# A two-layer relational graph convolution: layer 1's result kept in SBUF, transposed sums, and x and the output in rows of eight nodes

## The chip, the cores and the metric

The kernel runs on one core of a Trainium2 chip. The metric is the device time of one execution in microseconds. The median of three runs of the kernel before is 4638.85 us (4636.51 to 4646.56).

The core has five engines with a queue of instructions each: TensorE (PE, matmuls and weight loads), VectorE (DVE), ScalarE (ACT), GpSimd (POOL) and SyncE (SP). Here POOL does hardly anything but issue indirect DMAs (gathers of rows named by an index list), and SP issues nearly all other DMAs.

## The reference

`x` has 12500 nodes of 128 features. There are 200000 edges, sorted by their target `dst`, each with a source `src` and one of 8 relations. Two layers of a relational convolution are followed by a residual and a layer norm:

```python
def _rgcn_conv(x, src, dst, et, basis, comp, root, bias):
    W = jnp.einsum('rb,bio->rio', comp, basis)
    xw = jnp.einsum('ni,rio->nro', x, W)
    msgs = xw[src, et]
    seg = dst * N_REL + et
    summed = jax.ops.segment_sum(msgs, seg, num_segments=N_NODES * N_REL)
    cnt = jax.ops.segment_sum(jnp.ones((msgs.shape[0],), x.dtype), seg, num_segments=N_NODES * N_REL)
    mean = summed / jnp.maximum(cnt, 1.0)[:, None]
    agg = mean.reshape(N_NODES, N_REL, HIDDEN).sum(axis=1)
    return agg + x @ root + bias
...
    h = x
    for l in range(N_LAYERS):
        h_new = _rgcn_conv(h, src, dst, edge_type, basis[l], comp[l], root[l], bias[l])
        h_new = jax.nn.relu(h_new)
        h = h_new + h
    return h
...
x = _layernorm(x + _L0_gnn_ref(x, edge_index, edge_type_8, L0_gnn_basis, L0_gnn_comp, L0_gnn_root, L0_gnn_bias), axis=-1)
```

So each edge brings its source's row, times the weight of its relation, divided by the number of edges of that relation at its target.

## The kernel before, in words

**The plan.** `ordered_path` does the work (`general_path` stands by for edges whose distribution the first can't take; a flag read at the end chooses). It records every operation in program order in a `Plan` (lines 300 to 399), with the cells that it reads and writes. The plan derives the semaphore waits from these, and emits each engine's operations in that order. Nothing reorders them later: an engine that waits holds up all that is behind it in its queue. DMAs of SP, of ACT and of POOL's gathers use small sets of lanes (8, 4 and 3), and a DMA waits for the one before it on its lane.

**Sizes.** Nodes come in 98 blocks of 128 (`NT`), the last of 84. Edges come in 1563 tiles of 128. Four tiles make a quad (`Q`, 391 of them), eight a group (`G`, 196). A block of nodes has about 16 tiles, that is four quads or two groups. All data is fp32. A gather fetches the rows of one tile, so a quad is four gathers. Gathers are issued 12 quads ahead (`AHEAD`) into a ring of 14 slots `rows`; one-hot matrices two quads ahead, into a ring `dm` of 4.

**Layer 0.** For each quad `q` in turn: `gather` rows of x for quad q + 12 (line 577); `onehot` for quad q + 2 on DVE (line 863); `means` (line 903): PE multiplies the gathered rows with the one-hots, which are already divided by the counts, and ACT copies the result to `sT`. At even quads `product` of the group before (line 927): 16 PE passes through the weights of the eight relations, copied by ACT to `ys`. At odd quads `place` (line 950): PE adds the rows of `ys` into the sums `po` of the one or two blocks that they belong to. The sum of a block is opened by the root matmul in `open_block` (line 889), whose operand is x transposed: `load_block` loads 128 rows of x (64 KB), `turn_block` transposes them (line 882, bank `pt`) and ACT copies them to `hT`. When a block is complete, `close_block` adds the bias (line 963), takes the relu and adds x (line 964), and puts three items on a list `todo`: `turn` transposes the result on PE (line 970, bank `pt`), ACT copies it to `y_col`, and SP stores it to the DRAM tensor `hT_d`; `half(0)` and `half(1)` multiply it with the layer 1 weights of four relations each (line 975, bank `pt`), ACT copies to `y_row`, and the second stores 512 KB to the DRAM table `y_d`, which has a row for every node and relation. One item is taken from the list at three quads of four.

**Between the layers.** Layer 1 gathers from `y_d`, by node and relation, so its first gather waits for all stores to `y_d`.

**Layer 1.** Since the table holds products already, a quad takes one step, `add_rows` (line 1016): PE multiplies gathered rows and 256 wide one-hots into a transposed sum for two blocks; the root matmul (line 1019) is in it. `load2` fetches for each block its layer 1 input from `hT_d` to `h_in`, and its rows of x to `xs`. After a block's last quad `finish` lets ACT carry the half that belongs to the next block (line 1028, with the bias), and DVE adds the carry from before (line 1035) and does relu and residual (line 1036). One quad later `norm` transposes the block back on PE (line 1050); DVE adds x (line 1051), takes mean and variance (lines 1052 and 1053), ACT the root (line 1054), DVE the reciprocal and the scaling (lines 1056 and 1057), and SP stores 64 KB of output.

Names of lines 562, 565 and 577 in the profile are helpers: all loads and stores, all ACT copies, and all gathers.

Of the kernel before, what the change touches and what calls it, by code (L numbers as in the profile page):

```python
# [401 lines left out]
class Ring:  # L402


    def __init__(self, pool, n, shape, dtype, name):
        self.name, self.at = name, 0
        self.tiles = [pool.tile(shape, dtype, name=f"{name}{i}") for i in range(n)]
# [8 lines left out]
def ordered_path(  # L416
# [12 lines left out]
):  # L429

# [33 lines left out]
    assert D == P and R * K == P and B == BF + 1 and 1 < TL and LAST < P and BF % 4 == 0  # L464
# [9 lines left out]
    hT_d = dram.tile([NT * P, P], F32, name="hT_d")  # L474
# [9 lines left out]
    bias_sb = keep([P, D], F32, "bias_sb")  # L484
    bias_t = keep([P, 1], F32, "bias_t")
# [7 lines left out]
    dx = keep([P, B, C], I32, "dx")  # L493
    ex = keep([P, B, C], I32, "ex")
    src_i = keep([P, B, P], I32, "src_i")
    comp_sb = keep([P, L * R * NB], F32, "comp_sb")
    b_sb = keep([P, L, NB, D], F32, "b_sb")
# [9 lines left out]
    key = keep([P, 4, C], F16, "key")  # L507
    low = keep([P, 4, C], I32, "low")
    eqs = Ring(const, 2, [P, S4, 4, C], F16, "eq")
    turns = Ring(const, 3, [P, 4, P], F32, "tu")  # L510
# [5 lines left out]
    hin_r = Ring(const, 5, [P, D], F32, "h_in")  # L516
    hT_r = Ring(const, 3, [P, P], F32, "hT")
    h_r = Ring(const, 3, [P, D], F32, "h")
    yc_r = Ring(const, 3, [P, P], F32, "y_col")
    yr_r = Ring(const, 2, [P, R, D], F32, "y_row")  # L520
    xs_r = Ring(const, 4, [P, D], F32, "xs")
    st_r = Ring(const, 3, [P, nc.vector.BN_STATS_DIM + nc.vector.BN_AGGR_DIM + 1], F32, "st")
# [4 lines left out]
    po_b = [(psum.tile([P, D], F32, name=f"po{i}"), ("po", i)) for i in range(2)]  # L527
# [5 lines left out]
    v1 = keep([P, P], F32, "v1")  # L533
    v2 = keep([P, P], F32, "v2")
    v3 = keep([P, P], F32, "v3")
# [33 lines left out]
    def gather(l, q):  # L569
# [14 lines left out]
        if l == 1 and q == 0:  # L584
            reads += [("y_d", j) for j in range(NT)]
# [37 lines left out]
    def start():  # L623
# [26 lines left out]
        load(bias_sb, bass.AP(tensor=bias.tensor, offset=bias.offset, ap=[[0, P], [1, D]]), [], ["bias"], "ACT")  # L650
        load(bias_t, bass.AP(tensor=bias.tensor, offset=bias.offset + D, ap=[[1, P], [1, 1]]), [], ["bias_t"], "ACT")
# [127 lines left out]
    def check_edges(b):  # L779
        dxc = [("dx", b), ("dx", b, 1), ("dx", b, 2), ("dx", b, 3), ("pad", "dx")]  # L780
        for emit, r, wr in (
            (lambda: nc.vector.tensor_tensor(v1, dx[:, b, HALO + 1:HALO + P + 1], dx[:, b, main], op=ALU.is_lt),
             dxc, "v1"),
            (lambda: nc.vector.tensor_tensor(v2, dx[:, b, 2 * HALO:2 * HALO + P], dx[:, b, main], op=ALU.subtract),
             dxc, "v2"),
# [84 lines left out]
    def load_block(j):  # L870
        if j >= NT:
            return
# [151 lines left out]
    def finish(k):  # L1024
# [4 lines left out]
        if k < 0:  # L1029
            return  # L1030
# [199 lines left out]
```

## Time and profile before

| | before |
|---|---|
| median of three runs | 4638.85 us |
| the profiled execution | 4641.11 us |
| its span, first to last instruction | 4639.3 us |
| gathers of layer 0 | 3.4 to 2328.4 us |
| gathers of layer 1 | 2379.7 to 4591.5 us |
| PE busy | 2355.8 us (51%) |
| DVE busy | 1697.2 us (37%) |
| ACT busy | 502.0 us (11%) |
| POOL busy | 2962.0 us (64%) |
| bytes moved | 295.75 MB |

A row of the groups reads: line, engine, operation, what it writes from what it reads, number; busy time and mean length in ns of one; idle time of the engine just before them and what ended most of it. A row of the waits reads: engine, what waited, what released it, line of that; total in us, number, longest. "issue" is a gap with no wait that the profile shows, "remote" one with a releaser that it does not know. Ends of matmuls are modelled.

### The profile page before, as it was taken

The page shows a single profiled execution, that of the slowest core. Times are in us where ns is not written, and L with a number is a line of the kernel's source. Part 1 is how long each engine was busy: PE and PEld are TensorE (multiplying, and loading weights), DVE is VectorE, ACT ScalarE, POOL GpSimd, SP SyncE. Part 2 cuts the span into 40 slices and gives each one's busy share as a digit, 9 for nine tenths or more (in the row PEclk, how much of TensorE's full clock was granted, in tenths as well). Part 3 has the DMA queues.
Part 4 walks back from the last instruction along what each step waited for, and adds up shares of the span by engine and source line. Part 5 has one row for each costly group of instructions (what it writes and reads, how often), then busy time and mean ns, then how long its engine had stood idle before and what let it go on. Part 6 is the DMA issues. An engine that isn't in the chain of part 4 may idle for free.

```text
span 4639.3 us, 34983 instructions
## 1 busy us (share of the span) xinstructions
PE 2355.8 (51%) x11691; PEld 1911.0 (41%) x11691; DVE 1697.2 (37%) x4724; ACT 502.0 (11%) x1190; POOL 2962.0 (64%) x3134
## 2 busy tenths in 40 slices
PE   1675565556655565565563443444444344444444
PEld 1454555455544554454442332333333233333333
DVE  3874222222222232232232343434334343434434
ACT  0121111111111111121110000000000000000000
POOL 5466666666666666666646666666666666666663
PEclk9998888788788877788876776777777776767677
DMA  2122222222222222222221111211111111111121
GB/s 79 37 71 74 75 75 74 74 75 75 74 74 74 75 79 73 72 79 74 70 69 51 55 56 54 57 55 56 54 56 56 55 56 56 54 55 56 54 57 37
DMA packets 193392, 295.75 MB, mean 64 GB/s; under 512 B 60725, under 2 KB 130687, under 8 KB 193203
## 3 DMA queue, kind: packets, MB, share of 16 engines
q0 software_dynamic: 100032, 205.07, 15.6%
q1 hardware_dynamic: 90650, 86.62, 5.8%
q8 instruction: 96, 1.57, 0.1%
q10 hardware_dynamic: 2521, 1.73, 0.1%
q14 instruction: 93, 0.76, 0.1%
HBM read 229.18 MB, written 64.00 MB: 63 GB/s over the span
## 4 chain that ended last, share of the span: by engine, by line
another core or an unknown queue 38%; PE 26%; DVE 17%; issue 14%; ACT 3%; POOL 2%; DMA 0%; POOLq 0%; DVEq 0%; ACTq 0%; SPq 0%
DVE dm L863 12%; PE s L903 8%; PE y L927 6%; PE pt L975 4%; PE po L950 3%; POOL rows L577 2%; PE s L1016 1%; ACT sT L565 1%; DVE w_sb L597 1%; PE ct L705 1%; DVE eq L699 1%; PE ct L706 1%; DVE st L1052 1%; DVE ys L1057 1%
## 5 line engine op out<-in xcount | busy, mean ns | idle before, releaser
L577 POOL DMA_INDIRECT rows<-in_x_dram,idx x1563 | 1485.4, 950 | 841.0 <-issue 420.5
L577 POOL DMA_INDIRECT rows<-y_d,idy x1563 | 1475.5, 944 | 787.6 <-issue 419.0
L1016 PE MATMUL s<-dm,rows 128*128 128x256 f32 x2086 | 646.0, 469 | 595.1 <-DVE dm L863 482.0
L863 DVE TENSOR_SCALAR dm<-cols,near,w 128x256 f32<-128x256 f32 x1563 | 727.0, 533 | 255.3 <-remote 185.9
L1016 PEld LDWEIGHTS s<-dm,rows 128*128 128x128 f32 x2086 | 487.6, 245 | 710.3 <-DVE dm L863 499.6
L863 DVE TENSOR_SCALAR dm<-cols,kr,w 128x128 f32<-128x128 f32 x1563 | 525.9, 401 | 569.3 <-remote 348.1
L903 PEld LDWEIGHTS s<-dm,rows 128*128 128x128 f32 x3126 | 470.9, 222 | 121.9 <-issue 115.4
L903 PE MATMUL s<-dm,rows 128*128 128x128 f32 x3126 | 485.5, 305 | 6.1 <-issue 5.1
L950 PE MATMUL po<-ys,pl 128*128 128x128 f32 x780 | 167.6, 349 | 628.3 <-ACT ys L565 467.6
L927 PE MATMUL y<-w_sb,sT 128*128 128x128 f32 x3136 | 439.5, 300 | 65.4 <-issue 43.3
L1016 PE MATMUL ct<-dm,rows 128*128 128x256 f32 x1040 | 314.6, 457 | 291.1 <-DVE dm L863 216.7
L927 PEld LDWEIGHTS y<-w_sb,sT 128*128 128x128 f32 x3136 | 422.8, 216 | 75.1 <-issue 48.8
L950 PEld LDWEIGHTS po<-ys,pl 128*128 128x128 f32 x780 | 131.1, 239 | 656.4 <-ACT ys L565 486.9
L1016 PEld LDWEIGHTS ct<-dm,rows 128*128 128x128 f32 x1040 | 235.2, 237 | 347.7 <-DVE dm L863 224.7
L963 DVE TENSOR_TENSOR h<-po,bias_sb 128x128 f32<-128x128 f32 x98 | 28.5, 291 | 872.3 <-PE s L903 281.2
L1051 DVE TENSOR_TENSOR h<-po,xs 128x128 f32<-128x128 f32 x98 | 27.9, 285 | 816.6 <-remote 731.7
L565 ACT ACTIVATE sT<-s 128x512 f32<-128x512 f32 x391 | 233.8, 598 | 838.5 <-PE s L903 466.3
L975 PE MATMUL pt<-w_sb,y_col 128*128 128x512 f32 x392 | 254.1, 736 | 55.2 <-issue 31.2
L1050 PE MATMUL po<-ident,y_col 128*128 128x128 f32 x98 | 37.5, 383 | 379.8 <-DVE y_col L1036 185.3
L1050 PEld LDWEIGHTS po<-ident,y_col 128*128 128x128 f32 x98 | 15.4, 157 | 415.2 <-DVE y_col L1036 205.8
L1054 ACT ACTIVATE st<-st,eps 128x1 f32<-128x1 f32 x98 | 28.9, 294 | 1187.8 <-DVE st L1053 931.6
L565 ACT ACTIVATE y_row<-pt 128x512 f32<-128x512 f32 x196 | 117.0, 597 | 215.0 <-PE pt L975 95.2
(120 smaller groups left out, 1148.9 us busy)
## 6 DMA issues: line engine op xcount, KB each, us to landing
y_d<-y_row SPq DMA_DIRECT2D x97, 512.0 KB
rows<-in_x_dram,idx POOLq DMA_INDIRECT x1563
rows<-y_d,idy POOLq DMA_INDIRECT x1563
h_in<-in_x_dram SPq DMA_DIRECT2D x98, 64.0 KB
h_in<-hT_d SPq DMA_DIRECT2D x98, 64.0 KB
xs<-in_x_dram SPq DMA_DIRECT2D x98, 64.0 KB
hT_d<-y_col SPq DMA_DIRECT2D x97, 64.0 KB
out_dram<-ys SPq DMA_DIRECT2D x97, 64.0 KB
```

The lines of the kernel that those rows point to most:

```text
L565: act(lambda: nc.scalar.activation(out_t, in_t, AF.Copy), reads, writes)
L577: return [nc.gpsimd.indirect_dma_start(out=t[:, i - q * Q, :], out_offset=None, in_=x if l == 0 else y_d, in_offset=bass.IndirectOffsetOnA ...
L597: vec(lambda b=b: nc.vector.scalar_tensor_tensor(w_sb[:, l, r, :], b_sb[:, l, b, :], comp_sb[:, c0 + b:c0 + b + 1], w_sb[:, l, r, :], op0= ...
L699: vec(lambda s=s, eq=eq, s0=s0: nc.vector.tensor_tensor(eq[:, s - s0, :nb, HALO - s:HALO + P], key[:, :nb, HALO - s:HALO + P], key[:, :nb, ...
L705: nc.tensor.matmul(ct[:, :nb, :], id_h, eq[:, s - s0, :nb, main], start=(s == 1), stop=False)
L863: last = nc.vector.tensor_scalar(t[:, i - q * Q, :wide], cols[:, :wide], ids[:, i:i + 1], w[:, i:i + 1], op0=ALU.is_equal, op1=ALU.mult)
L903: last = nc.tensor.matmul(s[:, i, :], t[:, i, :], d[:, i, :P], start=True, stop=True)
L927: last = nc.tensor.matmul(y[:m], t[:, r, :nt, :].rearrange("p t k -> p (t k)"), w_sb[:, 0, r, :], start=(r == 0), stop=(r == R - 1))
L950: last = nc.tensor.matmul(po[j][0][:n], t[:m, k * P:k * P + n], o[:m], start=False, stop=(j in closed))
L975: pe(lambda: nc.tensor.matmul(pt[:n].rearrange("p r d -> p (r d)"), yc[:, :n], w_sb[:, 1, k * H:(k + 1) * H, :].rearrange("p r d -> p (r d)"),
L1016: ins = nc.tensor.matmul(a, t[:, i, :], d[:, i, :], start=(opens and i == 0), stop=(last and i == n - 1))
L1050: pe(lambda: nc.tensor.transpose(p[:n, :], v[:, :n], ident), [vc, "ident"], [pc])
```

## The change

**Layer 1's input stays in SBUF.** The DRAM tensor `hT_d` is gone. The result of layer 0, transposed, is written to `hT`, 98 x 128 columns of an SBUF tile `arena`. Tiles used only while the edges are prepared (basis weights, counting tiles, the source and target lists) lie in the same memory, and `h_cells` makes a write to `hT` wait for those it overlaps.

**Layer 0 sums transposed.** `place` takes `ys` as the stationary operand and the 256 wide placement matrix as the moving one, as `add_rows` does in layer 1; the root matmul is in it. `finish` serves both layers: ACT carries the second half on, DVE adds, takes the relu and adds the residual. In layer 0 it writes `hT`, so that there is no `turn`, `open_block` or `turn_block`, and `table` puts the two halves on the list.

**Eight nodes in a row.** x is read in 13 loads per layer with eight consecutive nodes in each partition (512 KB; the last group has two nodes in each of 106 partitions). `turn_x` transposes four slots into one bank and ACT copies them together. In layer 1 `finish` collects eight blocks in `wide`; `norm` takes them in two passes of four slots: four transposes into one bank, one DVE add, statistics, one root for four slots, scaling, and one store of 512 KB for the eight blocks. These are items of the list, one per quad.

**Order.** At the end of layer 0 the last steps stand in another order, and the last two blocks store each half by itself, with the second half in the bank `ct` and copied by DVE. A drain of POOL stands right behind the last gather. `check_edges` uses the ring `tu` in place of three tiles of its own, and both layers' biases are loaded as columns.

```diff
+    def turn_x(n, h):
+        p, k = shape_of(n)
+        t, c = xs[n]
+        if h == 0:
+            xT[n] = wide_r.take()
+        o, oc = xT[n]
+        pt, pc = pt_b
+        m = min(4, k)
+        def emit():
+            for s in range(m):
+                last = nc.tensor.transpose(pt[:, s, :p], t[:p, 4 * h + s, :], ident[:p, :p])
+            return last
+        pe(emit, [c, "ident"], [pc])
+        copy(by_slot(o, n)[:, 4 * h:4 * h + m, :], pt[:, :m, :p], [pc], [oc + (h,)])
...
     def place(g):
...
         def emit():
-            for k, j in pair(g):
-                n = rows_of(j)
-                last = nc.tensor.matmul(po[j][0][:n], t[:m, k * P:k * P + n], o[:m], start=False,
-                                        stop=(j in closed))
-            return last
+            ins = nc.tensor.matmul(a, o[:m], t[:m], start=opens, stop=last and not root_in)
+            if root_in:
+                ins = nc.tensor.matmul(a[:, :rows_of(k)], w_sb[:, 0, R, :], xt, start=False, stop=last)
+            return ins
+        pe(emit, reads, [ac])
+        if last:
+            n = finish(0, k)
+            if n is not None:
+                table(k)
+    def finish(l, k):
+        a, ac = acc.pop(k)
+        if k + 1 < NT:
+            nt, ncell = carry[k + 1] = carry_r.take()
+            act(lambda: nc.scalar.activation(nt, a[:, P:], AF.Identity, bias=bias_t[:, l:l + 1]),
+                [ac, ("bias_t", l)], [ncell])
...
+        vec(lambda: nc.vector.tensor_add(v[:, :n], a[:, :n], t[:, :n]), [ac, c], [vc])
+        vec(lambda: nc.vector.scalar_tensor_tensor(o, v[:, :n], 0.0, res, op0=ALU.max, op1=ALU.add),
+            [vc] + rc, oc)
...
-        def turn():
-            pe(lambda: nc.tensor.transpose(pt[:, 0, :n], h[:n, :], ident[:n, :n]), [hc, "ident"], [pc2])
-            copy(yc[:, :n], pt[:, 0, :n], [pc2], [ycc])
-            load(hT_d[j * P:(j + 1) * P, :n], yc[:, :n], [ycc], [("hT_d", j)])
...
-        todo.extend([turn, lambda: half(0), lambda: half(1)])
+        todo.extend([lambda: half(0), lambda: half(1)])
...
+        def add():
+            blocks_in = range(n * S, min(n * S + S, NT))
+            pe(emit, [vc + (j,) for j in blocks_in] + ["ident"], [bc])
+            vec(lambda: nc.vector.tensor_add(z, b[:p, :m, :], z), [bc, xc], [zc])
+        def stats():
+            for s in range(m):
+                vec(lambda s=s: nc.vector.bn_stats(st[:p, s, :A], z[:, s, :]), [zc], [sc + (s,)])
+            for s in range(m):
+                vec(lambda s=s: nc.vector.bn_aggr(st[:p, s, A:A + M], st[:p, s, :A]), [sc + (s,)], [sc + (s, 1)])
+            act(lambda: nc.scalar.activation(st[:p, :m, A + M], st[:p, :m, A + 1], AF.Sqrt, bias=eps[:p]),
+                [sc + (s, 1) for s in range(m)] + ["eps"], [sc + (9,)])
...
+        todo.extend([add, stats, scale] + ([store] if h == (k - 1) // 4 else []))
...
     g = NG - 1
-    for j in place(g - 1):
-        close_block(j)
-    product(g)
-    place_in(g)
     while todo:
         todo.pop(0)()
-    for j in place(g):
-        close_block(j)
+    place_in(g - 1)
+    product(g - 1)
+    place_in(g)
+    means(NQ - 1)
+    place(g - 1)
+    todo.pop(0)()
+    product(g)
+    todo.pop(0)()
+    place(g)
...
         gather(1, q + AHEAD)
+        if q + AHEAD == NQ - 1:
+            pool(lambda: nc.gpsimd.drain())
...
         add_rows(q, k, opens, last)
-        for d in due:
-            norm(d)
-        due = []
+        if todo:
+            todo.pop(0)()
         if last:
-            finish(k)
-            due.append(k)
-    for d in due:
-        norm(d)
+            finish(1, k)
+            n = k // S
+            if k >= 0 and (k % S == S - 1 or k == NT - 1):
+                for h in range(-(-shape_of(n)[1] // 4)):
+                    norm(n, h)
+                if n + 2 < NX:
+                    todo.append(lambda n=n: load_x(n + 2))
```

## The prediction

> **What bounds the kernel now.** I read the page first. The gathers on POOL are its two costliest groups:
>
> ```profile
> L577 POOL DMA_INDIRECT rows<-in_x_dram,idx x1563 | 1485.4, 950 | 841.0 <-issue 420.5
> L577 POOL DMA_INDIRECT rows<-y_d,idy x1563 | 1475.5, 944 | 787.6 <-issue 419.0
> ```
>
> One gather takes 0.945 us and 0.30 us of issue: a period of 1.2475 us. 1563 of them are 1950 us, twice 3900 us, of a span of 4639.3 us. The change issues the same gathers, so only the other 739 us can move: POOL's waits inside the layers, the gap between them, the tail. Next come the waits of POOL inside each layer, 300 to 2300 us and 2400 to 4590 us (engine, line, releaser: us in total, times, longest):
>
> ```profile
> POOL rows L577 <- issue: 376.2, 1231, 0.6
> POOL rows L577 <- remote: 186.9, 74, 3.4
> POOL rows L577 <- PE s L903: 93.7, 49, 2.7
> ```
>
> ```profile
> POOL rows L577 <- issue: 414.2, 1352, 1.5
> POOL rows L577 <- remote: 243.0, 71, 11.3
> ```
>
> With smaller rows, 1388 gathers fall in the first window: 2000 - 1388 x 1.2475 = 268 us of real waits, 3.1 us for each of its 86.75 blocks (16 gathers a block). The second has 1546: 2190 - 1928.6 = 261 us. Where the releaser is known it is TensorE, which frees a slot of the ring of 14 quads. So PE runs a full ring late, although it is hardly over half busy (start and end of the window, length, then busy us and instructions of PE, PEld, DVE, ACT, POOL; PEclk, DMA share, GB/s):
>
> ```profile
> 1000.00:1500.00 500.00, 297.32 (x1760) 256.43 (x1758) 144.65 (x440) 95.27 (x218) 327.83 (x348) 0.81 0.25 75
> 3500.00:4000.00 500.00, 218.90 (x774) 169.77 (x772) 200.66 (x510) 14.55 (x44) 332.95 (x354) 0.73 0.20 55
> ```
>
> The waits of PE between 300 and 2300 us say what makes it late in layer 0:
>
> ```profile
> PE po L950 <- ACT ys L565: 462.4, 69, 13.7
> PE po L950 <- issue: 160.6, 37, 12.3
> PE y L927 <- issue: 41.2, 27, 2.0
> PE po L889 <- issue: 37.0, 17, 4.8
> PE pt L975 <- issue: 31.2, 21, 2.2
> PE po L889 <- DVE h L963: 22.2, 13, 1.8
> PE y L927 <- ACT sT L565: 22.1, 17, 2.4
> PE po L889 <- ACT hT L565: 17.5, 18, 3.0
> ```
>
> Three quarters, 623 us, stand ahead of the place matmul L950, which waits for ACT's copy of the product; and ACT in turn waits for PE's product, "remote". In layer 1 (2500 to 4500 us) the long waits are DVE's, on PE's norm transpose:
>
> ```profile
> DVE h L1051 <- remote: 683.3, 39, 20.9
> DVE dm L863 <- remote: 172.1, 31, 15.7
> DVE y_col L1035 <- issue: 91.9, 25, 7.8
> DVE y_col L1035 <- ACT hT L1028: 91.5, 21, 9.8
> ```
>
> In the timeline at 3555 us the transpose L1050 starts at 3555.40 and the add L1051 behind it at 3576.66, when POOL has just stopped for want of a slot. The next one-hots stand behind that add in DVE's queue, and PE waits for them. Results of PE reach other engines up to 20 us late while gathers stream, and at once when they don't (after 4591 us, or between the layers). I cannot say why. I call it a hold. It costs POOL about 2.3 us every 12 gathers in layer 0 and 5.3 us every two blocks (49 times) in layer 1.
>
> **The Trainium skill.** "Perfetto Trace Analysis", Tensor Engine Instruction, says that the end of a matmul is estimated and its semaphore goes out once PSUM has acknowledged: this agrees with short gaps (0.4 us after L1050 at 4618.84), not with 20 us. "SBUF — State Buffer", Who interferes with whom, says that PE never waits on another engine, and that a DVE instruction with two SBUF inputs contends with a GpSimd instruction that reads SBUF. The trace doesn't lay the hold there: L1051 reads PSUM and SBUF and is held, L1036 with two SBUF inputs starts at 3555.00 unhindered among gathers. "DMA: Bandwidth & Descriptors", Anatomy of one DMA, gives a fixed cost of about 2 us apart from size: the last 512 KB store of y_d, issued at 2376.03, was there some 2.8 us later, before POOL resumed at 2379.74.
>
> **The change, part by part.**
>
> Layer 0, PE. Removed per block: the turn (L970, 0.27 us, with an ACT copy of 0.27 and a store to hT_d) and the wait for a private transpose of x ahead of the root matmul. The root matmul stays, inside place. Transposing x costs four transposes per bank in place of single ones: the same eight per eight blocks, but 2 ACT copies of 0.60 us in place of 8 of 0.27. Place becomes 2 passes of 256 columns (0.47 us each in the row of L1016, 128x256) in place of 4 of 128 (0.35): 0.94 against 1.40 us; as many columns pass, so I count none of it, and 0.46 x 86.75 = 40 us is the other end. Of the idle time, L889's rows go (37.0 + 22.2 + 17.5 and a row of 3.3: 80 us), and L882's two rows (10 us): 90 us in 86.75 blocks, 1.04 us. With L970 that is 1.3 us per block. The 53 us ahead of L975 stay, as half still needs the bank that ACT empties. If PE's lateness sets POOL's stops, 1.3 us per block off PE is 1.3 x 86.75 = 113 us at most. But the 623 us ahead of L950 stay, and a hold that met L889 can meet ys next. I take a third, -40 us; ends 0 and -153.
>
> Layer 0, ACT and DVE. ACT gains the carry (0.37 us, row L1028) and 0.15 us of wide copies, and loses 0.27 + 0.25: equal, at 95 us of 500. DVE has two instructions per block before and after, but its add now waits for ACT's carry too, as L1035 does in layer 1 (3.57 us there at 3554.68). One-hots for two quads ahead are queued behind it; PE would wait for them. Nothing taken: L963 waits for PE already, over 870 us of idle time before 98 instances, and PE has its dm two quads ahead. Without that cover 98 x 1 us.
>
> SP and DMA. Gone are the store to hT_d and its 98 loads, 196 loads of x become 26, 98 output stores become 13. SP's issues (0.32 to 0.43 us) lie on no chain except 3.3 us after 2376.03, which hold nothing. A 512 KB load of x lands 2 to 3 us after issue, estimated from the y_d store of that size, and is wanted eight blocks (180 us) later; it costs nothing, nor do y_d stores behind it in SP's queue wait, since its slot was read long before. At the very start 512 KB stand in the place of 64 KB, hidden by the counting before the first transpose; POOL is filled with 48 gathers (60 us) by then.
>
> Between the layers:
>
> ```profile
> 2370.30 0.29 DVE L963 TENSOR_TENSOR h<-po,bias_sb 84x128 f32<-84x128 f32 x1 [4.81 <-PE po L950]
> ...
> 2379.74 0.94 POOL L577 DMA_INDIRECT rows<-y_d,idy  x1 [51.38 <-DMA y_d<-y_row]
> ```
>
> From the end of the last means (2361.4) to the last y_d issue (2376.03) it is 14.7 us, with three items of block 96, place and three items of block 97 in series. After: product 1.95, ys 0.28, place 0.6, two DVE instructions 0.6, two halves 1.1 each, the DVE copy from the second bank 0.69 (a 128x512 operation), some 0.2 us at each of five handovers, and a half of block 96 between: 8.4 us. That is -6; ends 0 and -8.
>
> Layer 1. DVE's adds on PE's norm transposes go from 98 to 25, each with four slots. DVE per group of eight blocks: 2 x (0.69 + 4 x 0.295 + 4 x 0.182 + 0.164 + 4 x 0.349) = 8.3 us in place of 8 x 1.275 = 10.2; the 0.69 is bounded by 0.29 and 4 x 0.285 = 1.14. An item stands between two one-hots (1.89 us), at most 1.9 us long, in a quad of 4.99 us: hidden by the gathers, and if not, its sum is no more than before. hT in SBUF takes away loads that PE waits for nowhere. If the stops belong to the norm's add they fall to a quarter: 261 x 0.74 = -193 us. If the hold only needs any wait on PE, it meets the carry and L1035 of each block, held already up to 9.8 us, and nothing is gained. I take a quarter, -48; ends 0 and -193 here, and above nothing in the rival below.
>
> Tail. The last gather ends at 4591.5. What follows is DVE's: one-hots and norms to 4621.2, then the last store and SP's wait of 8.3 us for POOL's drain. The drain now stands right behind the last gather: -8 if it needs only POOL, 0 if it is as late; I take -7. Group 11's norm of 8.3 us falls into the tail where three blocks' norms (3.8 us) did: +4. Net -3; ends +4 and -8.
>
> Sum: the profiled run took 4641.1 us, 1.8 around its span. 4641.1 - 40 - 6 - 48 - 3 = 4544; the median of the runs shown is 2.3 us below the profiled one: 4542, and I say 4545.
>
> **Rivals.** *Held elsewhere (0.15).* The stops keep their number since any wait on PE will do. For: the first hold of layer 1, 43.3 us at L1035, came at a finish. Only gap and tail remain: 4639 - 9 = 4630, between 4620 and 4640.
>
> *Holds vanish with their waits (0.17).* For: 39 of the 49 long ones in layer 1 are at L1051, which nearly goes. Layer 1 gives 193, layer 0 half of 113: 4639 - 193 - 57 - 9 = 4380. Against: L950 keeps its wait.
>
> *Slower (0.18).* With the norm's add gone, DVE's first wait on PE is the finish, on the way to the carry, in every block and not in every second. A stop of 5.3 us at three blocks of four makes 74 stops for 49: +132, less 40 and 9: 4722; at every block (98): 4850. It decides from the point where the added stops eat 49 us: 49 / 5.3 = 9 more, 58 in all. Against: finishes are there now and mostly escape.
>
> **How the numbers follow.** Likeliest 0.47 (4490 to 4600 by itself), the rivals 0.15, 0.17 and 0.18, other 0.03. The range of 4390 to 4680 leaves out about half of the vanishing holds and over half of the slower case. No change is within 0.2% (9 us), about what a measurement of this kernel can tell. Faster: 0.47 + 0.17 + half of 0.15 + 0.02 = 0.73; same 0.08; slower 0.19.
>
> **What would show it.** Right: POOL's period still 1.2475 us; real waits of POOL in layer 0 near 230 us in 2000, above all still with place waiting for ys; in layer 1 near 210 us, with fewer long waits at the norm's add and longer ones at the finish's; the gap after the last gather of layer 0 at 45 us; no wait on an x load. Wrong: a gather of another length; a wait of POOL on the arena's early tiles or of PE on x; more than 58 stops in layer 1; or hardly any stop at all, which would say that waiting on PE with DVE's queue behind it is the whole cause.

## The result, and the profile after

The kernel after takes 4629.68 us (median of 12 runs, 4625.91 to 4640.26) for 4640.5 us before (12 runs). The ratio is 0.9979, with a 95% interval of 0.997 to 0.9988: 10 us (0.2%) faster, where I had forecast 95. The time lies inside the range, which was wide, but the mechanism that I took for likeliest did not happen. The rival "held elsewhere" gave 4630.

The profiled execution has a span of 4625.2 us, 14.1 less than before. From the starts and ends of the gathers in the trace it divides so:

| us | before | after | change |
|---|---|---|---|
| first to last gather, layer 0 | 2325.0 | 2330.5 | +5.5 |
| of this, POOL's real waits in the first 300 us | 92.4 | 99.2 | +6.8 |
| of this, POOL's real waits later | 271.8 | 270.7 | -1.1 |
| gap between the layers | 51.4 | 44.4 | -7.0 |
| first to last gather, layer 1 | 2211.8 | 2207.5 | -4.3 |
| of this, POOL's real waits | 260.6 | 255.8 | -4.8 |
| from the last gather to the end | 47.9 | 39.3 | -8.6 |

(A real wait is a gap between two gathers less the 0.30 us that every gap has.)

In the page of after, the groups of POOL's gathers, as busy time, mean ns of one, idle time before them:

```profile
L603 POOL DMA_INDIRECT rows<-in_x_dram,idx x1563 | 1485.2, 950 | 846.9 <-issue 417.3
L603 POOL DMA_INDIRECT rows<-y_d,idy x1563 | 1476.0, 944 | 775.8 <-issue 442.4
```

A gather is as long as before. POOL's waits of after in the same two windows, 300 to 2300 us and 2400 to 4590 us:

```profile
POOL rows L603 <- issue: 372.6, 1208, 0.6
POOL rows L603 <- remote: 205.7, 90, 3.4
POOL rows L603 <- PE s L954: 83.5, 59, 5.7
```

```profile
POOL rows L603 <- issue: 437.5, 1430, 0.6
POOL rows L603 <- remote: 259.5, 72, 9.8
```

With the smaller rows these are 1389 and 1546 gathers, so the real waits are 2000 - 1389 x 1.2475 = 267 us and 261 us, by the working that gave 268 and 261 before. (Some 4 us of the second lie behind the last gather, which ends at 4585.87.) They agree to a few us although the waits of the other engines have changed. PE between 300 and 2300 us:

```profile
PE po L1008 <- ACT ys L591: 552.3, 69, 14.7
PE po L1008 <- issue: 124.6, 35, 11.1
PE y L975 <- issue: 54.9, 39, 4.5
PE y L975 <- ACT sT L591: 38.4, 26, 3.1
```

The root matmul's own waits (80 us) are gone, and place (L1008) waits 677 us, 623 before. In layer 1, DVE between 2500 and 4500 us:

```profile
DVE dm L894 <- remote: 611.7, 57, 18.5
DVE v L1041 <- ACT carry L1024: 230.9, 30, 19.5
DVE x_g L1119 <- remote: 116.4, 13, 18.9
DVE v L1041 <- issue: 112.2, 28, 13.8
```

The norm's add (L1119), 683 us before, now waits 116 us. The one-hots (L894), 172 us before, wait 612. What left one row is in others, and POOL's sum is the same. Two of the same windows of after show the pace in one number, the x behind POOL's busy time, which is the fifth:

```profile
1000.00:1500.00 500.00, 294.53 (x1612) 252.88 (x1613) 140.46 (x428) 99.24 (x201) 327.17 (x348) 0.76 0.25 72
3500.00:4000.00 500.00, 236.43 (x761) 179.45 (x762) 192.46 (x484) 9.90 (x28) 331.86 (x352) 0.66 0.20 53
```

348 gathers in 500 us of layer 0 were 348 before; 352 in layer 1 were 354.

The end of layer 0 and of the kernel are where the time went. In the timeline of after:

```profile
2372.02 0.24 DVE L1041 TENSOR_TENSOR v<-po,carry 128x84 f32<-128x84 f32 x1 [0.32 <-PE po L1010]
...
2374.58 0.69 DVE L1059 COPY y_row<-ct 84x512 f32<-84x512 f32 x1 [2.04 <-PE ct L1054]
...
2378.39 0.94 POOL L603 DMA_INDIRECT rows<-y_d,idy  x1 [44.37 <-DMA y_d<-y_row]
```

From the first DVE instruction of the last block to POOL's restart it is 6.4 us, 9.4 before. In the tail (from the last gather to the end), DVE's last instruction ends 27.7 us after the last gather (29.7 before), and the 18.2 us after that are now 11.6: the drain of POOL that stood at 4623.57 before and took 8.48 us takes 0.04 us at its place now, since the new one has run by then.

### The profile page after: what moved, and what is told of

It reads as the page before. It is cut to its first block, busy times and chain, and to the rows that moved or that the text cites. A ratio compares the mean times of both kernels' runs of the same rounds, so it can differ in the third digit from the quotient of the medians.

```text
span 4625.2 us, 32936 instructions
## 1 busy us (share of the span) xinstructions
PE 2403.7 (52%) x11205; PEld 1929.6 (42%) x11205; DVE 1652.6 (36%) x4580; ACT 495.7 (11%) x1042; POOL 2962.3 (64%) x3134
## 4 chain that ended last, share of the span: by engine, by line
another core or an unknown queue 43%; PE 27%; issue 13%; DVE 13%; ACT 3%; POOL 2%; DMA 0%; POOLq 0%; DVEq 0%; ACTq 0%; SPq 0%
DVE dm L894 8%; PE s L954 8%; PE y L975 7%; PE pt L1054 4%; PE po L1008 3%; POOL rows L603 2%; PE ct L1091 2%; ACT sT L591 1%; PE s L1091 1%; PE ct L732 1%; DVE w_sb L623 1%; PE ct L733 1%; DVE arena L726 1%; ACT carry L1024 1%
## 5 line engine op out<-in xcount | busy, mean ns | idle before, releaser
L1091 PE MATMUL s<-dm,rows 128*128 128x256 f32 x2086 | 672.0, 479 | 811.2 <-DVE dm L894 518.4
L894 DVE TENSOR_SCALAR dm<-cols,near,w 128x256 f32<-128x256 f32 x1563 | 725.6, 533 | 829.6 <-remote 686.4
L894 DVE TENSOR_SCALAR dm<-cols,kr,w 128x128 f32<-128x128 f32 x1563 | 525.4, 401 | 493.4 <-remote 324.1
L1008 PE MATMUL po<-pl,ys 128*128 128x256 f32 x392 | 168.8, 521 | 698.0 <-ACT ys L591 566.9
L975 PE MATMUL y<-w_sb,sT 128*128 128x128 f32 x3136 | 463.3, 310 | 95.0 <-issue 54.9
L975 PEld LDWEIGHTS y<-w_sb,sT 128*128 128x128 f32 x3136 | 442.8, 225 | 110.7 <-issue 63.4
L1008 PEld LDWEIGHTS po<-pl,ys 128*128 128x128 f32 x392 | 74.3, 237 | 728.9 <-ACT ys L591 590.4
L1041 DVE TENSOR_TENSOR v<-po,carry 128x128 f32<-128x128 f32 x98 | 28.5, 291 | 932.2 <-ACT carry L1024 782.3
L1054 PE MATMUL pt<-w_sb,arena 128*128 128x512 f32 x388 | 239.8, 705 | 21.0 <-issue 8.9
L1024 ACT ACTIVATE carry<-s,bias_t 128x128 f32<-128x128 f32 x65 | 23.9, 368 | 1321.4 <-remote 1026.3
L591 ACT ACTIVATE ys<-y 128x128 f32<-128x128 f32 x196 | 54.2, 277 | 756.0 <-remote 526.8
L732 PE MATMUL ct<-arena,id_h 128*128 128x512 f16 (+1 forms) x188 | 70.9, 397 | 94.4 <-DVE arena L726 65.4
L1041 DVE TENSOR_TENSOR v<-s,carry 128x128 f32<-128x128 f32 x66 | 18.9, 286 | 274.8 <-ACT carry L1024 152.4
```

Of the source, the lines that this page charges most:

```text
L591: act(lambda: nc.scalar.activation(out_t, in_t, AF.Copy), reads, writes)
L732: nc.tensor.matmul(ct[:, :nb, :], id_h, eq[:, s - s0, :nb, main], start=(s == 1), stop=False)
L894: last = nc.vector.tensor_scalar(t[:, i - q * Q, :wide], cols[:, :wide], ids[:, i:i + 1], w[:, i:i + 1], op0=ALU.is_equal, op1=ALU.mult)
L975: last = nc.tensor.matmul(y[:m], t[:, r, :nt, :].rearrange("p t k -> p (t k)"), w_sb[:, 0, r, :], start=(r == 0), stop=(r == R - 1))
L1008: ins = nc.tensor.matmul(a, o[:m], t[:m], start=opens, stop=last and not root_in)
L1024: act(lambda: nc.scalar.activation(nt, a[:, P:], AF.Identity, bias=bias_t[:, l:l + 1]), [ac, ("bias_t", l)], [ncell])
```

## The experiments

All edits are to the kernel after unless the text says otherwise. The runs came in six sets, and the kernel before was timed in each: it took 4684, 4645 (one run), 4640, 3998, 4682 and 3994 us. The record names the chips 0, 0, 12, 13, 2 and 10 for them, so the chip number alone doesn't tell the first two apart. Absolute times of different sets aren't comparable. A run stands beside the before of its own set, and layers are compared by the pace of their gathers, that is the time from one gather's start to the next. "Gap" is the time between the layers, "tail" the time behind the last gather.

**The ends put back.** Four kernels ran in the first set, where before took 4683.93 us. The first gathers of layer 1 wait for whole blocks again, which isn't shown.

```diff
...
-    for q in range(NQ - 1):
+    for q in range(NQ):
...
+    place(g - 1)
+    product(g)
+    place_in(g)
     while todo:
         todo.pop(0)()
-    place_in(g - 1)
-    product(g - 1)
-    place_in(g)
-    means(NQ - 1)
-    place(g - 1)
-    todo.pop(0)()
-    product(g)
-    todo.pop(0)()
     place(g)
...
-        split = j >= NT - 2
+        split = False
...
-        if q + AHEAD == NQ - 1:
-            pool(lambda: nc.gpsimd.drain())
```

> The kernel after, with the two ends put back as they were: the order of the last steps of layer 0 and the unsplit last stores, and no drain of POOL right behind the last gather. If the ends are all that the change gains (held elsewhere), the gap between the layers is back near 50 us for 44, the tail near 48 us for 39, and the time within 5 us of the kernel before, 4640. If the work inside the layers had gained as I forecast, the time would stay 40 us or more below before.

Measured: gap 51.2 and tail 48.8 us, as before the change; 4676.40 us, ratio 0.9982 (0.9975 to 0.9989). The gap and the tail are what these edits gain. But 7.5 us below before was more than the 5 us that I allowed, so in that set the rest of the change gained something too, where the two first profiles show +1.2 us for the layers (5.5 - 4.3). There is no profile of before in that set to say where. That the ends are all of the gain is therefore not shown; that they are most of it in the profiled pair is.

**No norm.** In the same set. The store waits for x alone, which isn't shown.

```diff
...
-        todo.extend([add, stats, scale] + ([store] if h == (k - 1) // 4 else []))
+        todo.extend([store] if h == (k - 1) // 4 else [])
```

> The kernel after without the norm of layer 1: its transposes, add, statistics and scaling are left out, and what is stored is x. If the stops of POOL in layer 1 belong to DVE's waits on the norm's transposes, POOL's real waits there fall from 256 us to under 130. If any wait on PE meets the hold, they stay at 200 to 260 us, with the carry and the one-hots waiting.

Measured: real waits of 267.1 us in layer 1, with no norm there at all. DVE's waits from 2500 to 4500 us:

```profile
DVE dm L894 <- remote: 1084.2, 85, 19.9
DVE v L1041 <- ACT carry L1024: 92.6, 24, 5.6
```

DVE waits no less than before, nearly all of it at the one-hots. So the stops don't belong to the norm; I had counted a quarter of them as its own.

**A quarter of the bytes.** In the same set.

```diff
-                out=t[:, i - q * Q, :], out_offset=None, in_=x if l == 0 else y_d,
+                out=t[:, i - q * Q, :32], out_offset=None,
+                in_=(x if l == 0 else y_d).rearrange("n (a c) -> (n a) c", c=32),
...
+    for t, c in [rows_r.take() for _ in range(AHEAD + 2)]:
+        vec(lambda t=t: nc.vector.memset(t, 0.0), [], [c])
```

> The kernel after with gathers that fetch 32 of the 128 columns (128 bytes for 512, from a denser table; results are wrong): the same number of gather instructions and of descriptors, a quarter of the bytes. If the traffic of the gathered data is what delays PE's signals, POOL's real waits (370 and 256 us) fall by more than half and the time to 4300 or less. If it is the stream of gather instructions or of descriptors, they stay within 50 us of these.

Measured: 392.2 and 272.2 us of real waits, gathers of 950 and 944 ns. In its window 3000 to 3500 us (second line) POOL issues 352 gathers at 18 GB/s, before (first line) 354 at 55. The bytes aren't what sets the pace.

```profile
3000.00:3500.00 500.00, 221.27 (x781) 173.09 (x780) 200.10 (x512) 14.85 (x45) 333.48 (x354) 0.73 0.20 55
3000.00:3500.00 500.00, 215.66 (x764) 169.90 (x763) 185.65 (x470) 9.52 (x27) 331.27 (x352) 0.69 0.08 18
```

**PE reads something else.** In the same set.

```diff
-                last = nc.tensor.matmul(s[:, i, :], t[:, i, :], d[:, i, :P], start=True, stop=True)
+                last = nc.tensor.matmul(s[:, i, :], ident, d[:, i, :P], start=True, stop=True)
...
-                ins = nc.tensor.matmul(a, t[:, i, :], d[:, i, :], start=(opens and i == 0),
+                ins = nc.tensor.matmul(a, ident, d[:, i, :], start=(opens and i == 0),
```

> The kernel after with PE's matmuls on gathered rows reading the identity for the rows (the waits on the gathers stay, the results are wrong). If PE is late since its reads of the freshly written rows are slow, POOL's real waits fall by more than half. If its signals are late whatever it reads, they stay at 370 and 256 us within 50 us.

Measured: 387.3 and 269.3 us of real waits, where the last experiment has 392.2 and 272.2. PE's reads of fresh rows aren't it either. That everything taken away so far changed nothing pointed at the gathers themselves.

**Gathers that wait for nothing.** Before took 4644.59 us in this set. The matmuls are those of the last experiment, and the waits go too.

```diff
-        pe(emit, [c, dc], [sc])
+        pe(emit, [dc], [sc])
...
-        reads = [c, dc]
+        reads = [dc]
```

> The kernel after with PE not using the gathered rows at all: the matmuls read the identity in their place and don't wait for the gathers, and so no gather waits for PE to free a slot (results are wrong). If the stops of POOL come from PE's late signals, the gathers of a layer take 1950 to 1970 us with hardly a stop. If the gathers have a slower rate of their own, which the stops only show, a layer's gathers still take 2200 us or more, with the pauses at other waits or inside the instructions. It also shows PE's own pace through layer 0 while gathers stream, without any wait on them.

Measured: the gathers of layer 0 take 2165.6 us from first to last, those of layer 1 2161.0 us. Neither of my two figures was met exactly, but it is nearer the second theory: 2160 and not 1950, with hardly a stop, and the time inside the instructions. The page's groups of this kernel:

```profile
L603 POOL DMA_INDIRECT rows<-y_d,idy x1563 | 1664.5, 1065 | 1489.8 <-DMA y_d<-y_row 993.3
L603 POOL DMA_INDIRECT rows<-in_x_dram,idx x1563 | 1656.8, 1060 | 510.2 <-issue 485.2
```

The recorded gather has become longer, 1060 and 1065 ns for 950 and 944. Three windows of it (PE first, POOL the fifth pair):

```profile
3165.00:3285.00 120.00, 28.26 (x96) 21.78 (x95) 20.92 (x48) 1.10 (x3) 90.73 (x97) 0.60 0.18 53
3500.00:4000.00 500.00, 69.14 (x179) 47.63 (x180) 46.38 (x119) 3.73 (x8) 385.65 (x358) 0.55 0.17 49
2400.00:2900.00 500.00, 500.00 (x3726) 447.06 (x3725) 320.94 (x993) 230.57 (x460) 0.00 (x0) 1.00 0.15 59
```

After a rest, the first 97 gathers come at 120 / 97 = 1.24 us; in the trace this lasts for some 165. Later it is 358 in 500 us: 1.40 us each, with nobody to wait for. The 1.2475 us that I took for the period of a gather are those of a burst, and 1.40 us is the pace that a stream without waits keeps here. Against it a gather of the burst is 0.15 us early. The stops of the kernel before come to 268 / 1388 = 0.19 us per gather in layer 0 and 261 / 1546 = 0.17 us in layer 1, so with its stops it is hardly slower than a stream that waits for nobody.

One thing doesn't fit. The free stream makes some 165 gathers before it slows down, but in the kernel before POOL's first stop in layer 1 comes after 80 gathers, and with a ring of 4 slots (measured below) after 28; in both the first 100 gathers of the layer come at 1.38 us each. So the stops aren't just the end of that burst. That they are the stream's pace is argued from their sums.

The second and third windows show the other half: while gathers stream, PE, which waits for no gather here, is busy for 69 us of 500; when they are over, for 500 of 500, at the full clock. In part DVE and ACT hold it, for they get its results late: the copy of `s` at 1310.12 us starts 88 us after the end of the last matmul that it reads, and ACT has been idle for 66.6 us of them. In part PE's own instructions come slowly, with no wait that the profile shows:

```profile
1216.30 0.37 PE L954 MATMUL s<-dm,ident 128*128 128x128 f32 x1 [2.43 <-issue]
1217.70 0.29 PEld L954 LDWEIGHTS s<-dm,ident 128*128 128x128 f32 x1 [2.51 <-issue]
1219.10 0.37 PE L954 MATMUL s<-dm,ident 128*128 128x128 f32 x1 [2.43 <-issue]
1220.50 0.29 PEld L954 LDWEIGHTS s<-dm,ident 128*128 128x128 f32 x1 [2.51 <-issue]
1221.90 0.37 PE L954 MATMUL s<-dm,ident 128*128 128x128 f32 x1 [2.43 <-issue]
...
1310.12 0.60 ACT L591 ACTIVATE sT<-s 128x512 f32<-128x512 f32 x1 [66.59 <-remote]
```

They start 1.40 us apart, which is the period of the gathers.

**A ring of 8 slots.** In the same set.

```diff
-    AHEAD = 12
+    AHEAD = 6
```

> The kernel after with gathers issued 6 quads ahead into 8 slots in place of 12 into 14. If a hold ends because POOL stops, and POOL stops because the ring is full, the stops come about as often as holds begin and POOL's real waits grow by less than a fifth (370 to under 440, 256 to under 310 us). If the ring's depth is what carries POOL over PE's late signals, they nearly double.

Measured: 368.6 and 253.2 us of real waits, within 3 us of the first profile of after (369.9 and 255.8). The gap falls to 30.9 us and the tail to 31.0, and the time is 4606.68 us (one run). POOL can be at most 8 quads ahead of PE in place of 14, so less is left to do when the last gather of a layer ends.

**The measure for the next set.** Before took 4639.53 us there.

> The kernel after as it is, as the measure for the other kernels of this set. 0.3 to 0.2% faster than before; gap 44 us, tail 39 us.

Measured: 4630.84 us, ratio 0.9981 (0.9974 to 0.9988), gap 45.2 and tail 39.9 us.

**Half the rows.** In the same set.

```diff
-                out=t[:, i - q * Q, :], out_offset=None, in_=x if l == 0 else y_d,
-                in_offset=bass.IndirectOffsetOnAxis(ap=ids[:, i:i + 1], axis=0))
+                out=t[:P // 2, i - q * Q, :], out_offset=None, in_=x if l == 0 else y_d,
+                in_offset=bass.IndirectOffsetOnAxis(ap=ids[:P // 2, i:i + 1], axis=0))
...
+    for t, c in [rows_r.take() for _ in range(AHEAD + 2)]:
+        vec(lambda t=t: nc.vector.memset(t, 0.0), [], [c])
```

> The kernel after with gathers of 64 rows for 128 (the upper half of the indices is left out; results are wrong): as many gather instructions, half the descriptors. If the pace of the gathers is set by descriptors, the gather instruction gets shorter or POOL's real waits inside the layers fall by more than half. If it is set by the instruction itself or by PE's work and waits, which are all unchanged, they stay at 370 and 256 us within 50 us with gathers of 945 ns.

Measured, and expected by neither theory: the gather is shorter (905 ns for 946 in layer 1), the real waits are longer by as much (321.1 for 255.4 us), and the layer takes 2210.8 us where the kernel after beside it takes 2209.9.

```profile
L603 POOL DMA_INDIRECT rows<-y_d,idy x1563 | 1414.2, 905 | 843.4 <-issue 414.4
```

Whatever the instruction needs for itself, the pause makes up the rest to 2210.8 / 1563 = 1.414 us. The number of rows doesn't set the pace, nor does the recorded length of a gather.

**Rings of 6 and 4 slots.** In the same set, by the same edit with 4 and with 2.

> The kernel after with gathers 4 quads ahead (6 slots). If POOL's stops are the gather stream's own pace, they stay at 370 and 256 us within 30 us, and PE is fewer quads behind when the last gather of a layer ends: gap near 25 us for 44, tail near 25 for 39, some 33 us faster than after. If the ring carries POOL over PE's late signals, four quads (20 us) are too few for holds of 20 us and the stops grow by 100 us or more.

> The kernel after with gathers 2 quads ahead (4 slots, 10 us of gathers). The same question at the far end: with the stream's own pace the stops stay within 60 us and the time is 30 to 45 us below after; otherwise PE's latency from landing to freed slot is longer than two quads, the stops double and the kernel is slower than before by more than 200 us.

Measured: real waits of 370.1 and 257.7 us with 4, of 373.0 and 254.8 us with 2. The gap is 31.2 and 24.2 us, the tail 21.5 and 21.4. The times are 4597.29 us, ratio to before 0.9907 (0.9887 to 0.9927), and 4593.74 us, ratio 0.9898 (0.9877 to 0.9919). A ring of 4 slots carries POOL no worse than one of 14, so the depth of the ring buys nothing while a layer runs, and costs what PE has to work off after it. Both beat the kernels before and after of this set.

**Half the gathers.** This set ran where before takes 3997.74 us. The semaphore count of the gathers is changed to match, which isn't shown.

```diff
-                for i in range(q * Q, min((q + 1) * Q, T))]
+                for i in range(q * Q, min((q + 1) * Q, T), 1 if l == 0 else 2)]
...
```

> The kernel after with every second gather of layer 1 left out (782 for 1563; PE and DVE do all their work, on old rows for the missing ones, so results are wrong). If a gather instruction has a sustained pace of 1.40 us of its own, layer 1's gathers take 782 x 1.40 = 1095 to 1200 us, with the same 1.40 to 1.45 us each. If the pace was PE's, signals and waits per quad of 5.65 us, they take nearly as long as before, 2000 us or more.

Measured: 782 gathers in 976.4 us without a single stop, which is 1.2486 us each and under what both theories said. The layer 0 of the same run, unedited, has no stop after 300 us either. Here the burst is the pace, so the run doesn't decide the question.

**A short ring for the kernel before.** In the same set, an edit to the kernel before: `AHEAD = 2`.

> The kernel before with gathers 2 quads ahead for 12 and nothing else changed. If the gain of the short ring is in the gap and the tail alone and needs nothing of the change, its layers keep their 364 and 261 us of waits within 20 us and it is 25 to 40 us faster than before.

Measured: 4045.34 us, ratio 1.0126 (1.0109 to 1.0143), slower and not faster. There is no real wait in layer 1 and none in layer 0 after 300 us; in the first 300 us there are 77.9. With the deep ring the kernel after has 36 us there in the last set, where the gathers don't slow down either. So in such a set the deep ring is worth something at the start of layer 0; the 42 us between the two are most of the 48 us that the run lost.

**Again where gathers are slow.** This set ran where before takes 4682.43 us. The edits are those told above, and `AHEAD = 2` in the kernel before for the last.

> The kernel after, beside before, once more. Where the gathers come at 1.40 to 1.44 us on the mean, as in the profiles of before and after: ratio 0.998, gap 44, tail 39 us. Where they come at 1.2475 us without stops, as in the last set: gap and tail are all that can move again, 10 to 20 us faster than before unless the start costs something.

Measured: 4663.99 us, ratio 0.9956 (0.994 to 0.9973), better than the 0.998 that I expected, with a gap of 53.4 us and a tail of 39.8.

> The kernel after with PE not using the gathered rows and no gather waiting for PE (results are wrong). Where before takes 4640: gathers of 1.40 us and PE about 10% busy while they stream, as seen once. Where before takes 4000: if slow gathers and late signals are one thing, gathers of 1.2475 us, and PE as busy as its work asks for beside them.

Measured: as the first time. Gathers of 1063 and 1065 ns, layers of 2168 and 2162 us.

> The kernel after with every second gather of layer 1 left out (results are wrong). Where before takes 4640: 782 gathers at 1.40 to 1.45 us, 1095 to 1200 us in all, if the pace belongs to the gather instruction; 2000 us or more if it belongs to PE's work per quad. Where before takes 4000 it tells nothing on that, and takes the 976 us of the last set.

Measured: 782 gathers in 1135.9 us, 1.4526 us each. A window of its layer 1:

```profile
3000.00:3500.00 500.00, 371.27 (x1506) 301.80 (x1505) 371.28 (x945) 19.41 (x55) 323.24 (x343) 0.88 0.21 57
```

PE does 1506 matmuls and DVE 945 instructions in 500 us, where before did 781 and 512 in the same window (its line stands under A quarter of the bytes), and POOL issues 343 gathers for 354. PE and DVE can do all their work of layer 1 in 1136 us with stops and late signals. A gather takes 2% longer than in the kernel after beside it (2221.0 / 1563 = 1.421 us), with twice the work of PE per gather. So the pace goes with the gathers and not with PE's work per quad. This decides what was open.

> The kernel before with gathers 2 quads ahead. Where before takes 4640: 25 to 40 us faster than before by gap and tail, if the short ring needs nothing of the change and its layers keep their pace of 1.44 and 1.41 us. Where before takes 4000: slower by 1.3% as in the last set, by what the ring carries over at the start.

Measured: 4643.08 us, ratio 0.9917 (0.9901 to 0.9934), 39 us faster than before, with real waits of 388.0 and 274.1 us (383.6 and 265.2 in the kernel after beside it), gap 25.8, tail 27.9. The short ring needs nothing of the change.

**A deep ring at the start and a short one after.** Before takes 3993.81 us in this set.

```diff
+    LOW, DEEP = 3, 64
+    rows_lo = Ring(None, rows_r.tiles[:LOW + 2], None, None, "rows")
...
-        t, cell = rows_r.take()
+        t, cell = (rows_r if l == 0 and q < DEEP + AHEAD else rows_lo).take()
...
-        gather(0, q + AHEAD)
+        if q < DEEP or q + LOW >= DEEP + AHEAD:
+            gather(0, q + (AHEAD if q < DEEP else LOW))
...
-    for q in range(AHEAD):
+    for q in range(LOW):
         gather(1, q)
...
-        gather(1, q + AHEAD)
-        if q + AHEAD == NQ - 1:
+        gather(1, q + LOW)
+        if q + LOW == NQ - 1:
```

> The kernel after with gathers 12 quads ahead for the first 64 quads of layer 0, as before, and 3 quads ahead into 5 slots from then on and in layer 1. Where before takes 4640 or more: gap near 28 us, tail near 22 us, the layers' pace unchanged, ratio 0.990. Where before takes 4000: the start keeps its deep ring, so that the 1.3% that the short ring cost before isn't lost, and gap and tail are no worse: ratio 0.99 to 1.0. If the pace inside the layers depended on the ring, it would be slower than after.

> The kernel after on the same chip, to compare: 0.9956 to 0.9981 where before takes 4640 or more; where before takes 4000, gap and tail alone, 10 to 20 us faster than before.

Measured: 3991.70 us, ratio 0.9993 (0.9985 to 1.0002), and the kernel after 3991.30 us, ratio 0.9994 (0.9986 to 1.0002). In this set neither differs from before by more than can be measured, and the 10 to 20 us that I expected of gap and tail are not there. The short ring does no harm once the start has its deep one. What it gains where gathers are slow was measured with rings of 4 and 6 slots all through, not with this kernel. The kernel after here:

```profile
L603 POOL DMA_INDIRECT rows<-y_d,idy x1563 | 1475.1, 944 | 492.3 <-issue 409.3
```

```profile
3000.00:3500.00 500.00, 293.57 (x877) 208.23 (x878) 221.65 (x563) 11.59 (x33) 377.79 (x402) 0.77 0.20 60
```

402 gathers in 500 us are 1.244 us each, with no stop in layer 1. PE keeps up with them: the gap is 16.2 us and the tail 19.9 although the ring has 14 slots. Slow gathers and late results of PE came together in every set that has slow gathers, and were absent together in the two others: in layer 0 of the kernel after the copy of `s` starts up to 15.8 us after the last matmul that it reads (half of them over 2 us), and in the traces of these two sets never over 0.1 us.

## Why the prediction was wrong

**What bounds the kernel** is the step that failed. "Only the other 739 us can move" took 1.2475 us for the time of a gather, and the 268 and 261 us of stops for time that POOL gets back when PE is less late. 1.2475 us is the time in a burst. Where before takes 4645 us, a stream that waits for nobody needs 2165.6 + 2161.0 = 4327 us for the two layers (the gathers that wait for nothing), and the first profile of before has 2325.0 + 2211.8 = 4537. So 427 of the 739 us couldn't be had by taking waits away, and 210 were left inside the layers, 92 of them in the first 300 us. The 268 and 261 us are mostly the difference between burst and pace (1388 and 1546 times 0.1525: 212 and 236 us). POOL's stops end with a signal of PE, and the profile names PE; but without DVE's norm, with a quarter of the bytes, with other reads of PE and with shorter rings their sum stayed where it was, and with half the rows the time of the layer did.

**Layer 0, PE, -40 us**: +5.5 measured. The waits of the root matmul went, as stated (80 us to none), and place waits 54 us longer, as the sentence on a hold that meets ys next had it. The matmuls of place take PE 168.8 us for 167.6, so that counting none of their 40 us was right. The third of 113 us that I took was a choice without a measurement behind it. The first 300 us have 6.8 us more, where I had put nothing; what they come from isn't known.

**Layer 1, -48 us**: -4.3 measured. The long waits did leave the norm's add (683 to 116 us), and went to the one-hots (172 to 612 us); for the finish (L1041), where I expected them, 343 us stand for 183. With no norm at all the stops stay.

**Between the layers, -6**: -7.0 measured, but not all of it where I put it. From the end of the last means to the issue of the last store of y_d it is 9.9 us (2365.37 to 2375.30), where I had worked out 8.4 for 14.7. So the chain gave 4.8 us; 1.6 us came ahead of it and 0.6 behind it. The store that I took for 512 KB is one of 336 KB, since the last block has 84 rows: its last packet ended 2.6 us after the issue, and POOL restarted 3.7 us after it. SP issues it, while the section of the Trainium skill that I set beside it ("DMA: Bandwidth & Descriptors", Anatomy of one DMA) is about DMAs that GpSimd issues. No term of the sum rests on it.

**Tail, -3**: -8.6. The drain gave 6.6 us, near the 7 that I took. The norm of the last full group cost nothing where I had put +4: its items ran between one-hots, and DVE's end is 2.0 us earlier.

**The rivals.** "Held elsewhere" (4630) had the time, and its arithmetic of gap and tail alone. In part that is luck, for its reason was another: the stops keep their number since any wait on PE will do. The runs speak for another, though it is argued from the sums: the stops are how a stream of 1.2475 us in bursts keeps a pace of 1.41 to 1.44. The vanishing holds (4380) would have needed 4537 - 193 - 57 = 4287 us for the gathers of both layers, less than the 4327 of the free stream. Of the slower case nothing was seen: 64 stops of over 1 us in layer 1 for 83 before. I had counted 49 stops of 5.3 us, which the trace of before doesn't have, and named 58 as the point of decision; the sum of the waits would have been the right measure.

**What stays open.** Why the gathers have 1.40 us in some sets and 1.2475 in others, and why PE's results are late where they are slow, isn't shown by any run. That the two are one condition is argued from their coming together. Also open is what paces them to 1.44 us in layer 0 and 1.414 in layer 1 and not 1.40, and why the first stops come before the free stream would slow down. And in two sets the change gained something besides what the profiled pair shows: 7.5 us with the ends undone, and some 10 us beyond the tail's 8 in the set where it gained 18.

A third thing goes with these two. Where gathers are quick, the traces hold 16 semaphore updates for the landing of each gather (50001 for 3126 gathers in the kernel after of the last set). Where they are slow, the traces hold 12 to 27% of that number (10695 in before, 11649 in after, 5975 in the second run of the gathers that wait for nothing), and of PE's 1247 updates the trace of after holds 1105. So some of the waits named "remote" may be no more than an update that isn't in the trace. It also leaves a rival that no run tests: that the slow pace comes with the recording of these updates and not from the gathers alone. Every run on record has a span and a granted clock from the profiler, so none shows the kernel without it.

## What to carry to other kernels

Before stalls of a pacing engine are counted as time to be gained, measure its stream without anyone to wait for: if the free stream takes nearly as long as the one with its stalls, they are likely its pace, and removing what they wait for moves little. A ring deeper than the consumer's lag needs leaves more work to do at the end of each phase; here 4 slots for 14 gave 0.8% in sets with slow gathers, in both kernels (4593.74 for 4630.84 us, 4643.08 for 4682.43), and cost one of them 1.3% in a set without, where the waits that showed stood at the start of the first phase. And run such a kernel on more than one chip: before differed by 17% between the sets (4684 and 3994 us), more than any edit to it here gained. Count, too, how many of the expected signals a trace holds, before a wait is laid at an engine.

## What was not expected of the hardware

- A gather of 128 rows has a burst time of 1.24 to 1.25 us. In some sets a stream that waits for nobody keeps it for some 165 gathers after a rest and then has 1.40 us (two runs); in two sets the kernel itself has 1.25 us all through layer 1. Where it is slow, the kernel's pace of 1.41 to 1.44 us isn't changed by a quarter of the bytes (128 for 512 per row) or by half the rows, and hardly by half the gathers per unit of PE's work (1.45).
- While gathers stream at 1.40 us, a copy by ACT started 88 us after the result of PE that it reads, some of PE's instructions start 1.40 us apart, and PE is busy for 14% of the time where its work would fill all of it. The Trainium skill ("SBUF — State Buffer", Who interferes with whom) says that PE never waits on anyone. That is said of the ports of SBUF; no run here shows PE waiting for a port, and the late signals are something else. In two sets none of this appears.
- With rows halved in number the gather's record is 40 ns shorter and the pause after it longer by as much.
- POOL's drain took 8.48 us when it stood 32 us after the last gather. Queued right behind the last gather it ended 8.5 us after that gather's end, and the later one then took 0.04 us.
